# A four-layer conditioned transformer: two small norm operations from POOL to DVE, the norm's scalings on ACT seven pieces behind them, row transpositions nine pieces behind their load

## The chip, the cores and the metric

The kernel runs on one core of one Trainium2 chip, as one program that holds all four layers. Engines are called PE (TensorE), DVE (VectorE), ACT (ScalarE), POOL (GpSimd) and SP (SyncE, which issues most DMAs here). The metric is the device time of one launch in microseconds; the time before is the median of six runs. L12 is line 12 of the kernel before.

## The reference, cut to what matters

There are 4 batches of 512 tokens with 288 channels, and a condition vector for each batch. Each layer does the same two halves; the six modulation rows of a layer come from the condition.

```python
def layer(x, c, ...):                       # x (4, 512, 288), c (4, 288)
    mod = silu(c) @ ada_w + ada_b           # (4, 6 * 288)
    shift_a, scale_a, gate_a, shift_m, scale_m, gate_m = split(mod, 6, axis=-1)
    norm = lambda x: (x - mean(x)) / sqrt(var(x) + 1e-6)     # over channels
    h = norm(x) * (1 + scale_a) + shift_a
    x = x + gate_a * (attention(h) @ proj_w + proj_b)
    h = norm(x) * (1 + scale_m) + shift_m
    return x + gate_m * mlp(h)              # 288 -> 1152, gelu, -> 288
```

All layers have 16 heads of 18 channels. Layers 0, 1 and 3 attend over the 512 tokens of a batch. Layer 0 has four experts of which each token takes two; the others have a plain MLP. Layer 2 attends, inside each token, over its 16 heads, and then reads its result in another order:

```python
    attn = softmax(einsum("nthd,ntkd->nthk", q * scale, k))   # 16 x 16 in each token
    out = einsum("nthk,ntkd->nthd", attn, v)
    out = out.transpose(0, 2, 1, 3).reshape(n, t, d)          # heads before tokens
```

So a row of what goes into layer 2's projection holds parts of many tokens: the kernel writes the attention's result to memory and loads it back as rows.

## The kernel before, in words

**Tiles.** Tokens lie on partitions: 16 tiles of 128 tokens, four tiles (TB) for each batch b = 0 to 3; `x` with all of them stays in SBUF. For the products the normalised tokens are transposed into `ht`, channels on partitions: 3 chunks of 96 (first half of a layer) or 128 (second half).

**Planner.** The kernel writes down all engines' instructions in an order that it works out itself while it is built. PE's main work (steps of the attention, blocks of an MLP) is written by plain loops, which call `gap()` at set places. One gap is one turn of the planner: its clock `flow["now"]` goes one up, and in it side work is written down behind what stands there already. Side work is a Python generator; what it yields is a cost in us by the planner's own tables, or `WAIT` (no more of this generator in this turn; the text calls such a turn a piece behind), or `BANK` (it goes on when the turn's one free PSUM bank is its own). A wait of this kind is a place in the written order, not an instruction: each engine works off its queue in that order, and semaphores see to the rest. `mark(key, n)` says that a key counts as ready n turns on, and generators and loops wait for keys in turns as well.

**Where the change lies.** From 1298.1 us (the first L982), at the tail of layer 1's attention, layer 2's attention runs beside what is left of layer 1, the MLPs from 1327.3 us on (the first L1849). PE's loop is `half_mlp`: the MLPs of layer 1's batches 2 and 3 and then of layer 2's four batches, each batch in two halves of 256 tokens with 18 gaps a half (up L1849 and the remainder's channels, gelu L1860 on ACT, down L1871, then L1882 to L1884). Layer 2's MLP of batch b may begin only when its `ht` and the gate rows are there; until then the loop writes empty gaps:

```python
for b in range(B):
    while any(ready.get(key, 1 << 30) > flow["now"] for key in (("ht", 2, 1, b), ("gate", 2, 1))):
        gap(0.5)
```

Two lists are advanced once per gap by `follow()`, with a credit of 1.6 us a gap. `chain` is `stream()` in `attention_over_heads`: for 16 tiles in turn, products q, k, v of a tile (`kept`, matmuls L982 on PE, copy L991 on ACT), scores (`weigh`, DVE L1000 and L1006), maxima and shift (L1010 DVE, L1011 POOL), exponentials (L1155 ACT, of two tiles at once), sums of weights (L1034, L1035), values times weights (`weighted`, L1018, mostly on POOL), their sums (L1030 DVE), the division (L1043) and the write to memory (L1044, a DMA on SP). `beside` holds, for each batch, `before(b)`: the first norm of layer 2 and its chunks; and `after(b)`, which starts when batch b's last tile is written: `read(b)` (the DMA that loads the rows, and a memset on POOL), three transpositions of rows (`turned`, L1061 on PE, L1062 on ACT), four projections (`project`, L1068 PE, L1072 ACT, L1073 and L1074 POOL), and then the second norm and its chunks. A turn gives its bank to one of them, to `beside` before `chain`. Rows and the chunks' scratch tile share the buffers of `ht`; the normalised tokens `xh` have one buffer, which `norm` waits for in turns (`held`).

**The norm.** `norm(l, half, b)` takes statistics on DVE (L507, L508: one pair per tile), and has three forms. The form for layer 2 and for layer 3's first half (`scalar`) makes 1/sqrt(var + eps) and -mean/sqrt(var + eps) in four small operations on POOL over all four tiles at once (128x4 values), yields `WAIT` three times, takes `xh`, and then has ACT scale the four tiles (L532: `xh = x * rstd + off`). POOL then fills the columns behind the 288 (a copy L551 for second halves, a memset L556 for first halves), and `xh` counts as ready four turns on. The other form has DVE L522 for the eps, the same 128x4 operation as POOL's L515. `chunks` transposes `xh` on PE (L575) and modulates on ACT (L576). While layers 1 and 3 attend over tokens, the norms of batches go through another list, `lanes`, that has two turns per attention step. Twelve norms have the scalar form. Their first scalings begin at 1217.2, 1315.1 (layer 2, first half, batches 0 and 1), 1439.2 (the same, batch 2), 1489.3 (second half, batch 0), 1504.8 (first half, batch 3), 1571.6 (second half, batch 1), 1607.3 (layer 3, batch 0), 1658.3 and 1731.1 (layer 2, second half, batches 2 and 3), and 1812.2, 1826.1 and 1850.7 (layer 3, batches 1 to 3).

Other lines that the steps name: L264, L620 and L621 are memsets on POOL for layer 3's attention; the gate rows of layer 2's second half are loaded by one DMA and count as ready 8 turns after it is issued; L1407, L1717 and L1726 belong to layer 0's experts.

Of the kernel before, what the change touches and what calls it, by code (L numbers as in the profile page):

```python
# [12 lines left out]
ALU = mybir.AluOpType  # L13
# [16 lines left out]
EPS = 1e-6  # L30
# [29 lines left out]
def tile_dit_blocks(ctx: ExitStack, tc: tile.TileContext, x_in, cond_t, sel_den, sel_b, w_gate, layers, out):  # L60
# [14 lines left out]
    nc = tc.nc  # L75
# [28 lines left out]
    def mark(key, delay=1):  # L104
        ready[key] = flow["now"] + delay
# [395 lines left out]
    def norm(l, half, b):  # L501
        key = (l, half, b)
        n = f"{l}_{half}_{b}"
        mv = small.tile([P, TB, 2], F32, tag="mv", name=f"mv_{n}")
        for t in range(TB):
            st = small.tile([P, 6], F32, tag="st", bufs=4, name=f"st_{n}_{t}")
            nc.vector.bn_stats(st, x[:, b * TB + t, :])  # L507
            nc.vector.bn_aggr(mv[:, t, :], st)  # L508
            yield 0.6
        rstd = small.tile([P, TB], F32, tag="rstd", name=f"rstd_{n}")  # L510
        scalar = (l, half) in ((OVER_HEADS, 0), (OVER_HEADS, 1), (OVER_HEADS + 1, 0))
        if scalar:

            off = small.tile([P, TB], F32, tag="off", name=f"off_{n}")
            nc.gpsimd.tensor_scalar_add(rstd, mv[:, :, 1], EPS)  # L515
            nc.gpsimd.tensor_tensor(rstd, rstd, minus_half, ALU.pow)
            nc.gpsimd.tensor_tensor(off, mv[:, :, 0], rstd, ALU.mult)
            nc.gpsimd.tensor_scalar_mul(off, off, -1.0)
            for _ in range(3):
                yield WAIT  # L520
        else:
            nc.vector.tensor_scalar_add(rstd, mv[:, :, 1], EPS)  # L522
            nc.gpsimd.tensor_tensor(rstd, rstd, minus_half, ALU.pow)
        while held:
            yield WAIT
        held.append(key)
        xh[key] = work.tile([P, TB, CX], F32, tag="xh", bufs=1, name=f"xh_{n}")
        yield 0.0 if scalar else 0.6
        for t in range(TB):
            to = xh[key][:, t, :C]  # L530
            if scalar:
                nc.scalar.activation(  # L532
                    to, x[:, b * TB + t, :], AF.Identity, bias=off[:, t : t + 1], scale=rstd[:, t : t + 1]
                )
            elif (l, half) == (0, 1):

                add, scale = tokens_mod[b]
                nc.vector.scalar_tensor_tensor(
                    to, x[:, b * TB + t, :], mv[:, t, 0:1], scale, ALU.subtract, ALU.mult
                )  # L540
                nc.vector.scalar_tensor_tensor(to, to, rstd[:, t : t + 1], add, ALU.mult, ALU.add)
            else:
                nc.vector.tensor_scalar(
                    to, x[:, b * TB + t, :], mv[:, t, 0:1], rstd[:, t : t + 1], ALU.subtract, ALU.mult
                )
            if t < TB - 1:
                yield 0.1 if scalar else 0.6
        if (l, half) == (0, 1):
            pass
        elif half == 1:  # L550
            nc.gpsimd.tensor_copy(  # L551
                xh[key][:, :, C:].rearrange("p t (r c) -> p t r c", c=RC),
                xh[key][:, :, KF * P : C].unsqueeze(2).to_broadcast([P, TB, NR - 1, RC]),
            )
        else:
            nc.gpsimd.memset(xh[key][:, :, C : C + 1], 1.0)  # L556
        mark(("xh",) + key, 4 if scalar else 3)
        yield 0.1 if scalar else 0.6
# [40 lines left out]
    def attention(l, start):  # L599
# [298 lines left out]
        for b in range(B):  # L898
# [4 lines left out]
                lanes, start - 70 if first else at_step(s0 - LEAD - 9 if b else s0 - LEAD - 6),  # L903
                [("x", l, 0, b)] + ([("scattered", B - 1)] if l == 1 else []) + ([("step", l, 0)] if b else []),
                norm(l, 0, b),
            )
            free = [("first products", l, b - 2)] if b >= 2 else []
# [54 lines left out]
    def attention_over_heads(l):  # L962
# [83 lines left out]
        def read(b):  # L1046
            rows = work.tile([P, TB, C + 1], F32, tag="rows", bufs=1, name=f"rows_{l}_{b}")
            nc.sync.dma_start(
                rows[:, :, :C],
                scratch[b].rearrange("h t d -> (h t d)").rearrange("(n p c) -> p n c", p=P, c=C),  # L1050
            )
            nc.gpsimd.memset(rows[:, :, C : C + 1], 1.0)
            xh["rows", b] = rows

        def turned(b, k):
            if k == 0:
                rt[b] = work.tile([P, NK, S], F32, tag="ht", bufs=2, name=f"rt_{l}_{b}")
            n = KP + (1 if k == NK - 1 else 0)
            to = other()
            for t in range(TB):  # L1060
                nc.tensor.transpose(to[:n, t * P : (t + 1) * P], xh["rows", b][:, t, k * KP : k * KP + n], ident)  # L1061
            nc.scalar.copy(rt[b][:n, k, :], to[:n, :])  # L1062

        def project(b, t):
            pp = other()[:, :C]
            for k in range(NK):
                n = KP + (1 if k == NK - 1 else 0)
                nc.tensor.matmul(  # L1068
                    pp, rt[b][:n, k, t * P : (t + 1) * P], w["wp"][:n, k, :], start=k == 0, stop=k == NK - 1
                )  # L1070
            upd = work.tile([P, 2, C], F32, tag="upd", bufs=2, name=f"upd_a_{l}_{b}_{t}")
            nc.scalar.copy(upd[:, 0, :], pp)  # L1072
            nc.gpsimd.tensor_tensor(upd[:, 0, :], upd[:, 0, :], gates[l, 0][:, b, :], ALU.mult)  # L1073
            nc.gpsimd.tensor_tensor(x[:, b * TB + t, :], x[:, b * TB + t, :], upd[:, 0, :], ALU.add)  # L1074

        def until(*keys):
            while any(ready.get(key, 1 << 30) > flow["now"] for key in keys):
                yield WAIT

        def turn_normed(half, b):  # L1080
            yield from until(("mod", l, half), ("xh", l, half, b))
            turn = chunks(l, half, b)
            for k in range(NK):
                yield BANK
                next(turn)
                yield -0.9

        def before(b):

            yield from until(("x", l, 0, b))  # L1090
            if b >= 2:
                yield from until(("first products", l, b - 2))
            yield from norm(l, 0, b)
            yield from turn_normed(0, b)

        def after(b):

            for _ in range(3):
                yield WAIT
            read(b)  # L1100
            for _ in range(6):
                yield WAIT
            yield from until(("gate", l, 0), ("projection", l))
            for k in range(NK):
                yield BANK
                turned(b, k)
                yield -0.9
            for t in range(TB):
                yield BANK
                project(b, t)  # L1110
                yield -1.5
            mark(("x", l, 1, b), 4)
            yield from until(("x", l, 1, b))
            yield from norm(l, 1, b)
            yield from turn_normed(1, b)

        def stream():
# [13 lines left out]
            def second(behind=2):  # L1131

                k = at["weighted"]
                cost = 0.0
                if k < 4 * at["weighed"]:
                    if k % 4 == 0:
                        denominators(k // 4)
                        cost += 0.7
                    weighted(k // 4, k % 4)
                    at["weighted"] += 1  # L1140
                k = at["summed"]
                if k < at["weighted"] - behind:
                    summed(k // 4, k % 4)
                    at["summed"] += 1
                    cost += 1.4
                    if k % 4 == 3:
                        finish(k // 4)
                        if k // 4 % TB == TB - 1:
                            beside.append([after(k // 4 // TB), False])
                return cost  # L1150
# [992 lines left out]
```

## Time and profile before

| | |
|---|---|
| median of 6 runs | 2280.57 us (2274.94 to 2295.01) |
| the profiled execution | 2294.54 us |
| its span in the profile | 2292.5 us, mean granted TensorE clock 0.966 |
| PE | 2131.6 us busy, 93% of the span, 11018 matmuls |
| PEld | 1202.1 us, 52% |
| DVE | 1063.9 us, 46% |
| ACT | 807.2 us, 35% |
| POOL | 523.9 us, 23% |

A line of a timeline reads: start in us from the span's begin, duration, engine, line, operation, output and inputs by the program's tile names, their shapes, how many instructions were put together (x4), and in brackets how long the engine had stood idle before it and what ended that. PE is the matmuls, PEld the weight loads that overlap them. The slices of the page cut the span in 40 parts of 57.3 us; a digit is the busy share of one part in tenths. Matmul ends are modelled, so a PE that is shown busy is not one at its peak.

### The profile page before, as it was taken

The page shows a single profiled execution, that of the slowest core. Times are in us where ns is not written, and L with a number is a line of the kernel's source. Part 1 is how long each engine was busy: PE and PEld are TensorE (multiplying, and loading weights), DVE is VectorE, ACT ScalarE, POOL GpSimd, SP SyncE. Part 2 cuts the span into 40 slices and gives each one's busy share as a digit, 9 for nine tenths or more (in the row PEclk, how much of TensorE's full clock was granted, in tenths as well). Part 3 has the DMA queues.
Part 4 walks back from the last instruction along what each step waited for, and adds up shares of the span by engine and source line. Part 5 has one row for each costly group of instructions (what it writes and reads, how often), then busy time and mean ns, then how long its engine had stood idle before and what let it go on. Part 6 is the DMA issues. An engine that isn't in the chain of part 4 may idle for free.

```text
span 2292.5 us, 29720 instructions
## 1 busy us (share of the span) xinstructions
PE 2131.6 (93%) x11018; PEld 1202.1 (52%) x11018; DVE 1063.9 (46%) x1638; ACT 807.2 (35%) x1275; POOL 523.9 (23%) x553
## 2 busy tenths in 40 slices
PE   7889999999999999899999999989789999999998
PEld 3334434467775676344444566666556444443555
DVE  4546666540022212466535269898711455555111
ACT  2433434422221122445425322433312554445110
POOL 2001021230021120110001119898931200001000
PEclk9989999999999899999999989999989999999999
DMA  3243212346564463100000000210201100000000
GB/s 71 85 124 127 85 43 59 88 135 183 173 194 124 128 191 117 37 24 22 11 9 24 1 17 8 65 31 9 37 26 42 49 23 12 14 21 1 1 21 21
DMA packets 176066, 140.52 MB, mean 61 GB/s; under 512 B 83201, under 2 KB 157773, under 8 KB 175922
## 3 DMA queue, kind: packets, MB, share of 16 engines
q1 hardware_dynamic: 172654, 128.87, 19.8%
q0 software_dynamic: 3072, 9.44, 1.2%
q8 instruction: 88, 1.44, 0.3%
q14 instruction: 56, 0.46, 0.1%
q10 hardware_dynamic: 196, 0.31, 0.0%
HBM read 97.56 MB, written 26.29 MB: 54 GB/s over the span
## 4 chain that ended last, share of the span: by engine, by line
PE 63%; DVE 11%; POOL 4%; DMA 2%; issue 2%; ACT 2%; another core or an unknown queue 0%; SPq 0%; POOLq 0%; ACTq 0%; DVEq 0%
PE banks L705 12%; PE banks L634 7%; PE banks L1665 7%; PE banks L1645 6%; PE banks L1812 5%; DVE mx L715 4%; PE banks L1789 4%; PE banks L811 4%; PE banks L769 4%; PE banks L1871 2%; PE banks L1849 2%; POOL pv L1018 2%; DVE pq L1000 2%; PE banks L1651 1%; DVE ho L1030 1%
## 5 line engine op out<-in xcount | busy, mean ns | idle before, releaser
L715 DVE TENSOR_REDUCE mx<-banks 128x4 f32<-128x2048 f32 (+1 forms) x354 | 423.3, 1236 | 371.8 <-PE banks L705 343.8
L743 ACT ACTIVATE ex<-banks 128x1024 f32<-128x1024 f32 (+1 forms) x471 | 377.8, 865 | 360.0 <-PE banks L705 357.1
L705 PE MATMUL banks<-qk 32*128 32x512 f32 x3072 | 446.7, 633 | 52.7 <-DVE mx L715 18.4
L705 PEld LDWEIGHTS banks<-qk 32*128 32x128 f32 x3072 | 171.2, 187 | 227.6 <-issue 86.7
L1018 POOL TENSOR_TENSOR pv<-hs,qk 128x1152 f32<-128x1152 f32 x60 | 192.7, 3224 | 11.0 <-ACT hs L1155 11.0
L769 PE MATMUL banks<-ex,va 128*32 128x512 f32 x1536 | 191.9, 611 | 2.3 <-ACT ex L743 2.3
L1665 PE MATMUL banks<-w_b,hid_b 128*128 128x288 f32 x684 | 190.2, 423 | 0.0
L634 PE MATMUL banks<-ht,wqk 96*128 96x512 f32 (+1 forms) x348 | 172.4, 630 | 3.3 <-DVE mx L715 3.2
L1645 PE MATMUL banks<-block,w_b 128*128 128x256 f32 x684 | 166.0, 389 | 0.6 <-ACT hid_b L1657 0.6
L1657 ACT ACTIVATE hid_b<-banks,b_b 128x256 f32<-128x256 f32 x171 | 68.7, 471 | 273.8 <-PE banks L1651 164.7
L1665 PEld LDWEIGHTS banks<-w_b,hid_b 128*128 128x128 f32 x684 | 125.6, 193 | 55.3 <-issue 26.9
L1645 PEld LDWEIGHTS banks<-block,w_b 128*128 128x128 f32 x684 | 130.7, 195 | 28.2 <-issue 8.7
L794 POOL COPY rec<-r 128x512 f32<-128x512 f32 x48 | 29.9, 623 | 445.7 <-DVE r L790 431.5
L1871 PE MATMUL banks<-w,hid 128*128 128x288 f32 x432 | 128.5, 433 | 0.0
L1849 PE MATMUL banks<-ht,w 128*128 128x256 f32 x432 | 111.7, 393 | 17.8 <-ACT hid L1860 17.4
L769 PEld LDWEIGHTS banks<-ex,va 128*32 128x32 f32 x1536 | 39.9, 110 | 138.2 <-issue 69.4
L593 POOL TENSOR_TENSOR x<-x,upd_a 128x288 f32<-128x288 f32 x48 | 38.0, 793 | 322.0 <-DVE upd_a L592 307.8
L811 PE MATMUL banks<-wp,ot 128*128 128x288 f32 x384 | 106.3, 423 | 5.6 <-DVE mx L715 3.1
L1812 PE MATMUL banks<-w,hid 128*128 128x288 f32 x432 | 108.8, 410 | 0.0
L634 PEld LDWEIGHTS banks<-ht,wqk 96*128 96x128 f32 (+1 forms) x348 | 63.6, 194 | 83.6 <-issue 58.3
L1849 PEld LDWEIGHTS banks<-ht,w 128*128 128x128 f32 x432 | 82.1, 195 | 38.9 <-ACT hid L1860 22.2
L1789 PE MATMUL banks<-ht,w 128*128 128x512 f32 x216 | 97.2, 595 | 3.4 <-ACT hid L1805 2.3
(225 smaller groups left out, 2469.5 us busy)
## 6 DMA issues: line engine op xcount, KB each, us to landing
w_b<-in_w SPq DMA_DIRECT2D x57, 432.0 KB
w_b<-in_w SPq DMA_DIRECT2D x57, 384.0 KB
qk<-qc SPq DMA_DIRECT2D x316, 38.0 KB
wa<-in_wada SPq DMA_DIRECT2D x24, 288.0 KB
block<-x_mem SPq DMA_DIRECT2D x19, 288.0 KB
y_mem<-y_b SPq DMA_DIRECT2D x19, 288.0 KB
x_mem<-zeros SPq DMA_DIRECT2D x21, 256.0 KB
y_mem<-zeros SPq DMA_DIRECT2D x21, 256.0 KB
```

The costliest lines, as they stand in the source:

```text
L634: nc.tensor.matmul(to, st(rows, k), mv(rows, k), start=k == 0, stop=k == NK - 1)
L705: nc.tensor.matmul(to, qk[u][r, of, c * P : (c + 1) * P], qk[u][r, 1 - of, :], start=True, stop=True)
L715: nc.vector.tensor_reduce(mxs[u % 2][:, c, j : j + n], banks[:, bank + j : bank + j + n, :], AX.X, ALU.max)
L743: nc.scalar.activation(ex[step, j // 2][:, j % 2 : j % 2 + n, :], banks[:, to[j] : to[j] + n, :], AF.Exp)
L769: nc.tensor.matmul(to[j * HP : (j + 1) * HP, :], vas[0][:, c, at : at + HP], ex[step, j // 2][:, j % 2, :], start=first, stop=last,)
L811: nc.tensor.matmul(pp, done[b * NG + g][:, t * P : (t + 1) * P], w["wp"][:, g, :], start=g == 0, stop=g == NG - 1)
L1018: engine.tensor_tensor(prod, sc[i][:, hs, :].unsqueeze(2).to_broadcast([P, GH, HD, NH]), qkv[i][:, 1].rearrange("p h d -> p d h").unsqueez ...
L1645: nc.tensor.matmul(banks[:, UP + j, :BT], w1[:, k, j * P : (j + 1) * P], hx[i][:, k, :], start=k == 0, stop=False)
L1665: nc.tensor.matmul(banks[:, PY + t, :C], hid[j][:, t * P : (t + 1) * P], w2[:, j, :], start=f == 0, stop=f == NF - 1)
L1789: nc.tensor.matmul(banks[:, 4 + j, :], full[:, k, (f % 3) * P : (f % 3 + 1) * P], h[:, k, :], start=k == 0, stop=False,)
L1812: nc.tensor.matmul(banks[:, t, :C], hf[:, t * P : (t + 1) * P], w["w2"][f // 3][:, f % 3, :], start=f == 0, stop=f == NF - 1,)
L1849: nc.tensor.matmul(banks[:, UP + j, :BT], full[:, k, (f % 3) * P : (f % 3 + 1) * P], h[:, k, s], start=k == 0, stop=False,)
```

## The change

In the scalar form of the norm, the addition of eps goes from POOL to DVE. The sign change, which was done on the product on POOL, is now done on the mean, on DVE, before the product. POOL keeps the power and the product. Seven `WAIT`s instead of three stand between these operations and the four scalings on ACT. In `after(b)`, nine `WAIT`s instead of six stand between the load of the rows and their transpositions. Nothing else differs.

```diff
@@ norm, scalar form
-            nc.gpsimd.tensor_scalar_add(rstd, mv[:, :, 1], EPS)
+            nc.vector.tensor_scalar_add(rstd, mv[:, :, 1], EPS)
+            nc.vector.tensor_scalar_mul(off, mv[:, :, 0], -1.0)
             nc.gpsimd.tensor_tensor(rstd, rstd, minus_half, ALU.pow)
-            nc.gpsimd.tensor_tensor(off, mv[:, :, 0], rstd, ALU.mult)
-            nc.gpsimd.tensor_scalar_mul(off, off, -1.0)
-            for _ in range(3):
+            nc.gpsimd.tensor_tensor(off, off, rstd, ALU.mult)
+            for _ in range(7):
                 yield WAIT
@@ after(b)
             read(b)
-            for _ in range(6):
+            for _ in range(9):
                 yield WAIT
```

## The prediction

> **What bounds the kernel now.** I read the page's slices first. PE is near full throughout; DVE and POOL are full together only around slices 24 to 28, so the changed lines, which run from 1210 to 1852 us, matter mostly there.
>
> ```profile
> PE   7889999999999999899999999989789999999998
> DVE  4546666540022212466535269898711455555111
> POOL 2001021230021120110001119898931200001000
> ```
>
> Next, windows cut where PE's MLP work of batches starts and stops (columns: stretch, length, then busy time of PE, PEld, DVE, ACT, POOL, granted clock, DMA).
>
> ```profile
> 1436.00:1488.70 52.70, 48.01 (x217) 35.04 (x216) 43.16 (x50) 20.05 (x37) 45.38 (x35) 1.00 0.29 71
> 1488.70:1507.30 18.60, 11.36 (x42) 7.28 (x41) 18.29 (x24) 7.83 (x14) 17.11 (x13) 0.80 0.26 40
> 1507.30:1585.30 78.00, 74.34 (x313) 54.03 (x313) 72.43 (x72) 28.88 (x53) 73.85 (x45) 0.94 0.12 18
> 1585.30:1654.80 69.50, 59.54 (x255) 42.21 (x253) 51.65 (x61) 23.47 (x43) 62.49 (x47) 0.95 0.24 30
> 1654.80:1671.00 16.20, 7.85 (x19) 4.09 (x20) 10.57 (x8) 4.87 (x8) 15.22 (x17) 0.68 0.16 19
> ```
>
> From 1671 to 1797 PE works off the last two MLP batches alone, 119.36 of 126.00 us busy. So the stage ends when PE has done its work plus its pauses before 1671; rows two and five are the places where it has no MLP to do and waits for the norm of the next batch. Last, the engines' timelines: the scalings (L532) on ACT, and what PE shows behind them.
>
> ```profile
> 1439.19 2.19 ACT L532 ACTIVATE xh<-x,off,rstd 128x288 f32<-128x288 f32 x4 [3.25 <-POOL off L518]
> 1504.81 2.19 ACT L532 ACTIVATE xh<-x,off,rstd 128x288 f32<-128x288 f32 x4 [6.91 <-POOL off L518]
> 1571.64 2.19 ACT L532 ACTIVATE xh<-x,off,rstd 128x288 f32<-128x288 f32 x4 [6.67 <-POOL off L518]
> 1607.29 2.18 ACT L532 ACTIVATE xh<-x,off,rstd 128x288 f32<-128x288 f32 x4 [5.62 <-POOL off L518]
> 1658.31 2.19 ACT L532 ACTIVATE xh<-x,off,rstd 128x288 f32<-128x288 f32 x4 [8.38 <-POOL off L518]
> ```
>
> ```profile
> 1505.49 2.01 PE L575 MATMUL banks<-ident,xh 128*96 128x128 f32 x4 [3.93 <-ACT xh L532]
> 1574.54 1.82 PE L1849 MATMUL banks<-ht,w 128*128 128x256 f32 x4 [0.33 <-ACT hid L1860]
> 1609.89 1.13 PE L1849 MATMUL banks<-ht,w 128*128 128x256 f32 x4 [2.52 <-ACT hid L1860]
> 1616.29 1.09 PE L1061 MATMUL banks<-ident,rows 128*96 128x128 f32 x4 [3.48 <-DMA rows<-scratch]
> 1658.99 0.33 PE L575 MATMUL banks<-ident,xh 128*128 128x128 f32 x1 [4.23 <-ACT xh L532]
> ```
>
> ACT stands 31.0 us in six such waits. Behind L532 in its queue are the MLP's activations (L1860) and the copies L991, and PE then waits for those, or for xh itself.
>
> **Parts: the two operations.** In the six norms between 1436 and 1660 POOL loses L515 and L518, 0.31 and 0.23 us with the step between, 3.3 us in all. DVE gains two operations of 0.165 (L522, the same 128x4 form), 0.33 x 6 = 2.0 us; DVE is 93% busy in the third row, so I count them whole. They can be held: DVE's 128x288 TENSOR_SCALAR (L1717) took 0.36 us when it began first, and 1.51 when a POOL operation of 1.50 had begun.
>
> ```profile
> 665.26 1.51 DVE L1717 TENSOR_SCALAR outs<-outs,shares 128x288 f32<-128x288 f32 x1
> ```
> ```profile
> 665.10 1.50 POOL L1726 TENSOR_TENSOR x<-x,outs 128x576 f32<-128x576 f32 x1
> ```
>
> Behind POOL's products (L1018, 3.2 us) the hold per norm lies between 0 and 2 x 3.2. POOL itself sat waiting for DVE's statistics at three of the six L515 and had at most 0.6 us of other work left at the others, so I take 1.0 for all six. The page "SBUF — State Buffer" of the Trainium skill, "Who interferes with whom", makes a rule of it that speaks against this change: tensor_scalar on two ports and a GpSimd operation exclude each other for the whole instruction. By the rule's worst order at every norm the six would cost DVE 38 us.
>
> **The scalings.** A gap is one turn of the planner. A half MLP has 18 gaps and took 36.7 us (its first ones-products at 1388.51 and 1425.17), 2.04 us each; the wait of row two is 13 gaps, 1.43 each. Four gaps more are 8.2 us inside the MLP and 5.7 in a wait: more than every ACT stall except the 6.91 (1.2 left) and, barely, the 8.38. What goes: pauses of 1.66 (1443), 2.52 (1609) and 1.1 (1572, four short ones and 0.33), and at 1574 matmuls at half speed (L1849 x4 1.82 against 1.03; six groups, 3.5 over): 8.8. In row two 3.93 and (2.01-0.60)+(1.91-1.03) of slow matmuls: 6.2. In row five 4.23+0.38: 4.6. The page "TensorE: Matmul & The Clock Gate", Part 1, puts the slow clock behind an idle window of about 3.4 us; the pauses at 1572 were shorter, so by it the 3.5 would not be the scalings' and the gain would be 3.5 less. The slow rows directly behind them decide for me.
>
> **The row transpositions.** read() and its DMA stay where they are; only L1061 goes three gaps back, 6.1 us. Pauses 1.48, 0.34 and 3.48 (5.3); I take 4.5, since the third batch's row load shares SP's queue with the next layer's weights. Also, DVE idles 8.89 us before 1475.04, until L982: tile 8's three products stand behind the seven bank pieces of after(0) (three transpositions, four projections, PE 1456 to 1471). Batch 2's chunks end at the fourth gap later than now, and two gaps then remain before those seven: tile 8 fits in, tile 9 waits instead. Between 0 and 8.9; I take 3.0, since the exponentials (L1155) move back with tile 9.
>
> **What is late next.** From the projection to the next MLP: x counts as written after 4 gaps, statistics 1 or 2, waits 3 (now 7), 1 to take xh, 4 until xh counts, 3 chunks, 1. Row two ends not with that but with the gate load, 8 gaps after x; the chunk has 5 gaps of slack, so 7 later is 2 beyond: 15 gaps. Batch 1 has no slack now (no pause at 1585): 7 later less those 2 is 5. Batch 2: own chain 7 later, MLP start 7 later: 4 gaps become 3 or 4. Sum +6 gaps at 1.43 = 8.6. PE pays for these only if it runs out of other work; half of them hold L982 and transpositions that move there, but I count all. At the end POOL's copy L551 falls behind the memsets L264, L620 and L621 (3.61+1.15+0.21); less the 3.3 saved, 1.7.
>
> **Attention stages.** For the norms at 1210 and from 1803 on, four more turns are two steps, some 10 us. The chunks at 1820.84 go to about 1831 and the first two products of batch 1 into the same step; its keys are needed some 20 us on. Nothing on POOL stalls ACT there. Counted at zero; if the cover is short, one wait for a spread, 8.0 us (DMA qk<-qc at 1674.70).
>
> **Sum.** Gains 8.8+6.2+4.6+4.5+3.0 = 27.1; costs 8.6+2.0+1.0+1.7 = 13.3, and 0.8 for what is left of the two longest stalls: 13.0 net. The profiled execution was 2294.54 (span 2292.5), 14.0 above the median 2280.57; there it would give 2281.5. Off the median: 2267.5.
>
> **Rivals.** (1) The waiting is only handed on. DVE is 18.29 of 18.60 busy in row two and POOL 15.22 of 16.20 in row five; if these engines' own chain, not ACT's order, sets when xh is there, the 6.2+4.6+3.0 don't come: -13.0+13.8 = +0.8, near 2281; with half, 2274. For it: POOL itself waits 21.6 us at L515 for statistics. Against: ACT's stalls ended in L1849 pauses inside the MLP, where nothing needed the norm yet. (2) Slower: the gaps become the wait. If the chain of batch 1 keeps its order against PE, PE stands out 7 gaps (2+5) at the MLP's 2.04 us, +14.3, and nothing of rows two and five returns, while 8.8+4.5 inside the MLP is lost again to copies (L991) that now come before POOL has freed their tile; 2294.9. It decides when PE reaches the first chunk of batch 1 with xh unwritten by more than 6 us; for it, the zero slack at 1585; against, PE reaches that point earlier than now only by what it gained. (3) It doesn't do what it says: DVE's pair held at each norm by 3.2, 19 us on a full DVE; that eats the gain, 2280 or so.
>
> **Numbers.** A measurement of this kernel can tell about 0.5%, 11.4 us, from no change. Stalls go and most of it is kept: 0.62, of it 0.44 beyond 11.4 (own range 2256 to 2277). Rivals 1 and 3 together: 0.23, of it 0.19 within, 0.02 on either side. Rival 2: 0.15, of it 0.13 slower. Faster 0.46, same 0.39, slower 0.15. Low 2253: all gains, half the gaps hidden (4.3), tile 8 wholly (5.9), -23 and some noise of the median. High 2291: most of rival 2.
>
> **What would show it.** Right: L532 waits under 3 us in all where there were 31.0; L1061 waits under 1.5 where 5.3; no slow group near 1574; PE before the last two batches done some 13 us sooner; the pause before the first chunk of MLP batch 1 (now none) 2 to 5 us. DVE's two operations near 0.17 and not 1 to 3. Wrong: that pause over 8 us, or L991 waiting for L1018 on POOL by over 15 us between 1436 and 1660.

## The result: 0.73% slower, and the profile after

The change runs at 1.0073 of the time before, with a 95% interval of 1.0055 to 1.0092, so it takes about 16.7 us more (the two medians, 2303.47 us and 2284.56 us, lie 18.9 apart). The forecast was 2267.5 us, 13 us less, and its range ended at 2291.0.

The profiled execution took 2300.54 us (span 2298.8, clock 0.963). The two spans differ in layer 0's experts by chance: the 1281st score product (L705) comes at 974.37 us before and at 963.67 after, with nothing of the change ahead of it. I therefore count from a product that both have behind all that, the 1793rd L705 (1187.64 and 1176.97 us). From there to the end it is 1104.9 us before and 1121.9 after, 17.0 more, close to the 16.7 of the ratio. In three steps, each from the start of one instruction to the start of the other: to the last sum of layer 2's attention on DVE (L1030) 478.8 and 477.2; from there to the last down product of layer 2's MLP (L1871) 129.3 and 138.5; from there to the 2561st L705, in layer 3's attention, 151.7 and 161.1. The rest is 345.1 and 345.2. So DVE's chain beside the MLPs ends as early as before, PE needs 9.2 us more from there to its last down product, and layer 3's attention takes 9.4 us more.

The slices of the page after:

```profile
PE   7889999899999999899999898798789899999998
DVE  4545566540022214466443389789530455565111
POOL 2001021230021120110010159788811100001000
```

DVE and POOL are full at the same place as before, and PE's digits there have two 7s where there was one. Windows cut as in the prediction at the starts and stops of PE's MLP work (the same columns; the fifth row is the pause before layer 2's third MLP batch, the sixth the last two batches):

```profile
1421.00:1475.30 54.30, 50.67 (x214) 37.35 (x214) 43.05 (x40) 20.91 (x39) 47.75 (x29) 0.91 0.32 71
1475.30:1497.00 21.70, 6.76 (x18) 4.32 (x19) 21.18 (x36) 6.67 (x12) 16.64 (x14) 0.58 0.09 28
1497.00:1572.00 75.00, 71.94 (x318) 53.51 (x317) 65.56 (x69) 28.31 (x53) 65.99 (x39) 0.96 0.10 16
1572.00:1664.70 92.70, 72.00 (x264) 48.58 (x263) 69.36 (x74) 26.46 (x49) 79.67 (x60) 0.83 0.23 34
1664.70:1688.50 23.80, 14.10 (x45) 7.58 (x43) 4.14 (x7) 3.29 (x5) 0.00 (x0) 0.71 0.08 29
1688.50:1792.60 104.10, 104.10 (x470) 72.23 (x470) 14.23 (x30) 26.61 (x56) 19.17 (x19) 1.00 0.14 42
```

Length less busy time is PE's idle time: 3.6, 14.9, 3.1, 20.7, 9.7 and 0.0, in all 52.0 us. Before, the five rows and the last stretch had 4.7, 7.2, 3.7, 10.0, 8.4 and 6.6, in all 40.5. The second row doubled, and so did the fourth, batch 1's MLP.

A longer pause is not yet a loss, though. Counted from the first mark, layer 2's MLP of batch 0 starts at 319.7 us before and at 320.0 after, and that of batch 1 at 397.7 and 395.0: row two begins 2.7 us sooner than before and holds 4.6 us less work, and nothing is late at its end. The time is lost behind that, between the start of batch 1's MLP and that of the third (483.3 us before, 511.6 after). PE idles 30.4 us there where it idled 18.3. About 15 us more of that stretch is other work done sooner: from the third MLP on, PE has 104.1 us of work left in place of 119.4.

ACT's waits, from the view of waits between the first L982 and the last L1871 (columns: who waits for whom, us in total, times, longest):

```profile
ACT qk L991 <- POOL pv L1018: 20.9, 7, 8.4
ACT upd_a L1072 <- POOL x L1074: 14.9, 2, 8.2
ACT xh L532 <- POOL off L518: 7.9, 1, 7.9
ACT upd_m L1882 <- POOL x L1074: 5.1, 1, 5.1
ACT hs L1155 <- POOL hs L1011: 5.0, 4, 2.2
```

The scalings' wait that the prediction was built on fell from 31.0 to 7.9 us. But ACT waits for POOL still: with a last group of 2.7 (L991 for L556) these are 56.5 us, and the same view before has 60.4 (31.0 for L518, 11.6 and 10.8 in the first two groups, 7.0 in four small ones). The waits of PE in the same stretch:

```profile
PE banks L1849 <- ACT hid L1860: 25.5, 6, 11.6
PE banks L575 <- POOL xh L551: 7.8, 1, 7.8
PE banks L705 <- ACT qc L660: 6.3, 1, 6.3
PE banks L575 <- ACT xh L532: 6.1, 1, 6.1
PE banks L705 <- DMA qk<-qc: 3.4, 2, 3.2
```

Before, L1849 waited for the gelu 11 times, 17.4 us together and never over 2.8; now six times, with one of 11.6. How that one comes about is to be read from the engines' timelines, ACT first, then POOL and PE:

```profile
1623.44 0.40 ACT L1072 COPY upd_a<-banks 128x288 f32<-128x288 f32 x1 [8.15 <-POOL x L1074]
1630.59 0.40 ACT L1072 COPY upd_a<-banks 128x288 f32<-128x288 f32 x1 [6.75 <-POOL x L1074]
1632.30 0.84 ACT L1860 ACTIVATE hid<-banks,b 128x256 f32<-128x256 f32 x2
```

```profile
1623.37 3.13 POOL L1018 TENSOR_TENSOR pv<-hs,qk 128x1152 f32<-128x1152 f32 x1
1626.45 0.68 POOL L1043 TENSOR_TENSOR ho<-ho,hd 128x288 f32<-128x288 f32 x1
1627.09 0.80 POOL L1073 TENSOR_TENSOR upd_a<-upd_a,gate 128x288 f32<-128x288 f32 x1
1627.96 2.60 POOL L1074 TENSOR_TENSOR x<-x,upd_a 128x288 f32<-128x288 f32 x1
```

```profile
1632.83 3.48 PE L1849 MATMUL banks<-ht,w 128*128 128x256 f32 x8 [11.58 <-ACT hid L1860]
1681.82 2.04 PE L705 MATMUL banks<-qk 32*128 32x512 f32 x2 [3.20 <-DMA qk<-qc]
1683.79 1.54 PE L575 MATMUL banks<-ident,xh 128*128 128x128 f32 x6
```

The third batch's projections have two tiles `upd` for their copies, and POOL frees one only with L1074, behind its products L1018. The gelu of batch 1's MLP stands on ACT behind the waiting copies, and PE behind the gelu. The last two lines are the start of the third MLP: its chunk (L575) stands on PE behind layer 3's first score products, and these wait for the spread's DMAs. In the kernel before, the gelu that follows the third batch's projections, and the first of layer 3's score products, read

```profile
1638.63 2.79 PE L1849 MATMUL banks<-ht,w 128*128 128x256 f32 x8 [2.37 <-ACT hid L1860]
1684.40 1.12 PE L705 MATMUL banks<-qk 32*128 32x512 f32 x2
```

and the third MLP's chunk came ahead of that L705, at 1658.99.

### The profile page after: what moved, and what is told of

It reads as the page before. It is cut to its first block, busy times and chain, and to the rows that moved or that the text cites. A ratio compares the mean times of both kernels' runs of the same rounds, so it can differ in the third digit from the quotient of the medians.

```text
span 2298.8 us, 29740 instructions
## 1 busy us (share of the span) xinstructions
PE 2124.4 (92%) x11018; PEld 1200.0 (52%) x11018; DVE 1071.6 (47%) x1662; ACT 806.4 (35%) x1274; POOL 518.0 (23%) x529
## 3 DMA queue, kind: packets, MB, share of 16 engines
q1 hardware_dynamic: 172654, 128.87, 19.6%
## 4 chain that ended last, share of the span: by engine, by line
PE 63%; DVE 12%; POOL 3%; issue 2%; DMA 2%; ACT 2%; another core or an unknown queue 0%; SPq 0%; POOLq 0%; DVEq 0%; ACTq 0%
PE banks L705 12%; PE banks L1665 7%; PE banks L634 7%; PE banks L1645 6%; PE banks L1812 5%; DVE mx L715 4%; PE banks L1789 4%; PE banks L811 4%; PE banks L769 3%; PE banks L1871 3%; PE banks L1849 2%; DVE pq L1000 2%; DVE ho L1030 2%; POOL pv L1018 2%; PE banks L1651 1%
## 5 line engine op out<-in xcount | busy, mean ns | idle before, releaser
L705 PE MATMUL banks<-qk 32*128 32x512 f32 x3072 | 446.1, 632 | 58.4 <-DVE mx L715 19.2
L705 PEld LDWEIGHTS banks<-qk 32*128 32x128 f32 x3072 | 171.0, 186 | 235.9 <-issue 87.5
L1018 POOL TENSOR_TENSOR pv<-hs,qk 128x1152 f32<-128x1152 f32 x60 | 190.6, 3189 | 8.8 <-ACT hs L1155 8.8
L634 PE MATMUL banks<-ht,wqk 96*128 96x512 f32 (+1 forms) x348 | 170.3, 624 | 3.3 <-DVE mx L715 3.2
L1665 PEld LDWEIGHTS banks<-w_b,hid_b 128*128 128x128 f32 x684 | 124.0, 190 | 52.9 <-issue 25.1
L1849 PE MATMUL banks<-ht,w 128*128 128x256 f32 x432 | 114.4, 401 | 26.3 <-ACT hid L1860 25.5
L1871 PE MATMUL banks<-w,hid 128*128 128x288 f32 x432 | 129.5, 435 | 0.0
L1849 PEld LDWEIGHTS banks<-ht,w 128*128 128x128 f32 x432 | 84.9, 201 | 47.3 <-ACT hid L1860 28.3
L634 PEld LDWEIGHTS banks<-ht,wqk 96*128 96x128 f32 (+1 forms) x348 | 62.9, 192 | 83.1 <-issue 57.1
```

The costliest lines, as they stand in the source:

```text
L634: nc.tensor.matmul(to, st(rows, k), mv(rows, k), start=k == 0, stop=k == NK - 1)
L705: nc.tensor.matmul(to, qk[u][r, of, c * P : (c + 1) * P], qk[u][r, 1 - of, :], start=True, stop=True)
L1018: engine.tensor_tensor(prod, sc[i][:, hs, :].unsqueeze(2).to_broadcast([P, GH, HD, NH]), qkv[i][:, 1].rearrange("p h d -> p d h").unsqueez ...
L1665: nc.tensor.matmul(banks[:, PY + t, :C], hid[j][:, t * P : (t + 1) * P], w2[:, j, :], start=f == 0, stop=f == NF - 1)
L1849: nc.tensor.matmul(banks[:, UP + j, :BT], full[:, k, (f % 3) * P : (f % 3 + 1) * P], h[:, k, s], start=k == 0, stop=False,)
L1871: nc.tensor.matmul(banks[:, PY + t, :C], hf[:, t * P : (t + 1) * P], w["w2"][f // 3][:, f % 3, :], start=False, stop=f == NF - 1,)
```

## The experiments

All ratios are to the kernel before, measured beside each other, with 95% intervals. The last four columns come from each kernel's profile, in us, with the marks used above: to the last L1030, on to the last L1871, on to the 2561st L705, and from the first mark to the end. One profile is one execution: the last column goes with the ratio to about 5 us in every row but e_dve's, which is 7.2 us longer than before's where the ratio says 2.3 shorter.

| kernel | ratio | L1030 | L1871 | L705 | to the end |
|---|---|---|---|---|---|
| before | 1 | 478.8 | 129.3 | 151.7 | 1104.9 |
| the change | 1.0073 [1.0055, 1.0092] | 477.2 | 138.5 | 161.1 | 1121.9 |
| e_dve | 0.9990 [0.9975, 1.0004] | 484.9 | 127.7 | 154.3 | 1112.1 |
| e_r9 | 0.9988 [0.9974, 1.0002] | 479.0 | 129.7 | 151.7 | 1105.4 |
| e_w7 | 1.0079 [1.0057, 1.0100] | 485.2 | 134.8 | 159.1 | 1124.6 |
| e_dve_w7 | 1.0087 [1.0065, 1.0110] | 484.3 | 135.8 | 159.1 | 1124.3 |
| e_dve_r9 | 0.9982 [0.9969, 0.9995] | 478.5 | 128.6 | 152.4 | 1104.7 |
| e_l3only | 0.9993 [0.9981, 1.0004] | 478.3 | 126.2 | 158.4 | 1108.1 |
| e_h1only | 1.0036 [1.0023, 1.0049] | 479.8 | 139.4 | 151.7 | 1116.1 |
| e_h0only | 0.9968 [0.9954, 0.9981] | 476.2 | 127.8 | 152.3 | 1101.5 |
| e_l2only | 1.0044 [1.0029, 1.0060] | 479.0 | 139.8 | 151.7 | 1115.6 |
| e_pair | 1.0077 [1.0055, 1.0099] | 477.5 | 142.0 | 161.0 | 1125.7 |
| e_h0_pair | 0.9986 [0.9973, 1.0000] | 476.2 | 127.7 | 152.4 | 1101.4 |
| e_h0_h1w1 | 1.0023 [1.0007, 1.0039] | 477.1 | 137.4 | 151.7 | 1111.4 |
| e_hold | 1.0046 [1.0029, 1.0064] | 477.3 | 136.4 | 159.2 | 1118.0 |
| e_holds | 1.0046 [1.0030, 1.0061] | 477.4 | 134.8 | 160.0 | 1117.4 |
| e_holds_pair | 1.0047 [1.0029, 1.0064] | 477.5 | 134.7 | 160.0 | 1117.4 |
| e_h0_30 | 0.9966 [0.9954, 0.9979] | 476.3 | 126.0 | 151.7 | 1099.1 |
| e_copy | 1.0057 [1.0022, 1.0091] | 477.5 | 138.9 | 157.6 | 1119.1 |
| e_three | 1.0017 [0.9988, 1.0046] | 478.5 | 133.8 | 154.2 | 1111.8 |

**Each edit alone.** Edits against the kernel before: e_dve has only the four lines of the operations, e_w7 only the first of these lines, e_r9 only the second, e_dve_w7 the operations and the first.

```diff
-            for _ in range(3):      # norm, ahead of the scalings
+            for _ in range(7):
-            for _ in range(6):      # after(b), behind read(b)
+            for _ in range(9):
```

> Only the two operations on DVE; three turns before the scalings and six before the row transpositions, as before. Theory 1 (the time comes from the written order: the turns put copies on ACT and a copy on POOL behind other work; the operations themselves cost 0.33 us a norm): 0 to 3 us faster than before, L532's waits for POOL's product fall from 31.0 by some 3 us, MLP batch starts unchanged. Theory 2 (the two operations stand in DVE's full queue, and POOL's power now waits behind them): 10 us or more slower, POOL's waits for DVE at the power over 10 us above those of before.

> Only the seven turns before the scalings; the four operations on POOL and six turns before the row transpositions as before. Theory 1: 8 to 18 us slower: the pause before layer 2's first MLP chunk grows from 6.5 to about 14 us since POOL's copy into xh (L551) stands behind the next norm's operations, the copies L991 wait for POOL's products over 15 us, and layer 3's attention takes some 9 us more. Theory 2: within 5 us of before.

> Only the nine turns between row load and row transpositions. Theory 1: 3 to 10 us slower, with PE idle about 10 us more behind the third batch's projections, whose copies on ACT (L1072) wait for POOL's x (L1074); layer 3's attention unchanged. Theory 2: 0 to 5 us faster, from L1061's 5.3 us of waits for the rows.

> The whole change except that six turns stay before the row transpositions. Theory 1: slower than before by what seven turns alone cost, less 0 to 3 us: 6 to 16 us. Theory 2: slower by 10 us or more, the same as the two operations alone. If nearly all of the change's cost of about 17 us is in the nine turns, this one is within 5 us of before.

The two operations on DVE come out 0.10% faster and the nine turns 0.12%; neither interval excludes 1. Seven turns alone cost 0.79%, the whole of it. Theory 2, DVE's queue, is out. Theory 1 had the seven turns right, though e_dve_w7 is some 20 us slower where it allowed 16, and the nine wrong. In e_r9 no L1061 waits for the rows any more (11.1 us in the line's view before), and the time is 0.12% less: the pauses of 5.3 us on PE came back elsewhere, L532 waits 40.2 us there where it waited 31.0, and L1849 waits 21.1 us for the gelu where it waited 17.4.

**By norm.** The base is e_dve_r9 (operations and nine turns, three turns at the norms); the others give seven turns to one group of norms.

```diff
-            for _ in range(3):
+            for _ in range(7 if l > OVER_HEADS else 3):                # e_l3only
+            for _ in range(7 if half == 1 else 3):                     # e_h1only
+            for _ in range(7 if l == OVER_HEADS and half == 0 else 3): # e_h0only
+            for _ in range(7 if l == OVER_HEADS else 3):               # e_l2only
```

> Two operations on DVE and nine turns before the row transpositions, but three turns before the scalings as before: the base of the next three. Alone these parts gave ratios of 0.9990 and 0.9988. If they add up: 0.9978, some 5 us faster than before. If nine turns gain only by cover that the two operations also use up: 0.999.

> As the base (two operations on DVE, nine turns), with seven turns for layer 3's first norms only, three for layer 2's. Theory A (part of the cost is the norms inside layer 3's attention, where four turns more put chunks and key products behind two further steps): 7 to 10 us above the base, of it 7.5 to 9.4 between the end of layer 2's last MLP and the 2560th score product, and PE's idle time there near 10 where before had 7.4. Theory B (that stretch is longer because of what the MLP stage leaves over for it): within 3 us of the base.

> As the base, with seven turns for layer 2's second norms only (the ones that the next MLP waits for). Theory C (the MLP waits for the longer chain: xh later, MLP start later by four turns a batch): 8 us or more above the base, the pauses at the MLP starts grow, the copies L991 wait for POOL's products no longer than before (11.6 us). Theory D (the first norms move tile products in front of POOL's products): within 3 us of the base.

> As the base, with seven turns for layer 2's first norms only. Theory C: within 3 us of the base, or faster, since nothing of the MLPs waits for these norms. Theory D: 6 us or more above the base, the copies L991 wait for POOL's products over 20 us where before had 11.6, and the pause near the start of the second half of layer 1's last MLP is about 7 us where it was 2.8.

> The whole change, with layer 3's norms back at three turns. The whole stood at 1.0073 of before. If layer 3's turns cost in the whole what its trace shows between the last MLP of layer 2 and the 2560th score product (160.6 us against 151.3 to 152.0 where layer 3 has three turns): 6 to 9 us less, 1.0033 to 1.0047, and that stretch back at 151 to 152 us. If they cost only the 2.5 us by which they alone stood over the base: 1.006.

The second norms of layer 2 cost 0.54% over the base, 12 us; in the profiles it is 11.4, of it 10.8 between the last L1030 and the last L1871. That is theory C's size, but not its account: L991 waits 19.1 us for POOL in e_h1only, where C had it no longer than the 11.6 of before. Layer 2's first norms come out 0.14% below the base, within the intervals, although the first pause that Theory D named is there (6.80 us) and L991 waits 16.2 us for POOL: D is out. Layer 3's turns cost 6 us inside the attention and gain 2.4 in front of it; in the whole change the attention's stretch is 161.1 us with them and 151.7 without (e_l2only), and the ratios differ by 0.29%, 6.6 us. What the attention pays for is on PE after, 35 us into it:

```profile
1829.78 1.46 PE L705 MATMUL banks<-qk 32*128 32x512 f32 x2 [2.00 <-DMA qk<-qc]
1831.17 3.23 PE L769 MATMUL banks<-ex,va 128*32 128x512 f32 x16
```

The chunks of batch 1 come two steps later (L575 41.7 us behind the last L1871 in place of 25.1), new pauses of 0.63, 0.64 and 2.00 us appear before score products and a transposition of maxima, and behind the last one the same 16 value products that take 1.92 us elsewhere take 3.23: the granted clock is 0.66 between 1830 and 1835. Of the 9.4 us between 151.7 and 161.1, 2.7 are something else: twelve products at the start of that stretch ran at a slow clock, behind pauses that both kernels have (the last section has the lines). e_l3only has no such slow products and stands at 158.4; e_dve and e_three have them with three turns, and stand at 154.3 and 154.2.

**The longest pause taken away.** Against the change (e_pair) and against e_h0only (e_h0_pair), two projections share a tile, so the copies have four places:

```diff
-            upd = work.tile([P, 2, C], F32, tag="upd", bufs=2, ...)
-            nc.scalar.copy(upd[:, 0, :], pp)
+            if t % 2 == 0:
+                xh["pair", b] = work.tile([P, 2, C], F32, tag="upd", bufs=2, ...)
+            upd = xh["pair", b]
+            nc.scalar.copy(upd[:, t % 2, :], pp)
...                                  # POOL's two operations on upd[:, t % 2, :]
```

> The whole change; besides, two projections of a batch share one tile of two rows, so that ACT's copies L1072 have four places where they had two, and no longer wait for POOL's x (L1074) of two projections before. Theory E (the 11.58 us pause behind the third batch's projections is on the path): 5 to 12 us faster than the whole change, 1.002 to 1.005 of before, that pause under 4 us. Theory F (POOL and DVE set the pace there, and PE waits later for what it gains): within 3 us of the whole change, 1.006 to 1.0085.

> The fastest kernel so far (two operations on DVE, nine turns, seven turns for layer 2's first norms only; 0.9968) with the same shared tiles. Theory E: 3 to 8 us faster than that, 0.9935 to 0.9955, since L1072 waited 18.8 us for POOL there and PE stood 1.80 and 3.23 us behind it. Theory F: 0.996 to 0.998.

Theory E is out in both. e_pair lies in theory F's range; e_h0_pair is a little slower than F had it. PE in e_pair, whose lines behind this edit have numbers two higher:

```profile
1606.10 1.99 PE L1851 MATMUL banks<-ht,w 128*128 128x256 f32 x8 [0.73 <-ACT hid L1862]
1614.94 1.33 PE L1870 MATMUL banks<-b,ones 1*128 1x288 f32 x4 [6.21 <-ACT upd_m L1884]
1655.46 2.04 PE L705 MATMUL banks<-qk 32*128 32x512 f32 x2 [10.25 <-DMA qk<-qc]
1661.32 2.46 PE L705 MATMUL banks<-qk 32*128 32x512 f32 x4 [3.82 <-ACT qc L660]
1666.52 2.04 PE L705 MATMUL banks<-qk 32*128 32x512 f32 x2 [2.73 <-DMA qk<-qc]
```

The 11.58 became 0.73. The wait for the third batch's rows, ahead of it, grew from 3.30 to 7.35. Nine us behind it PE waits 6.21 for the next copy behind the same POOL, and at the third MLP's start 16.8 where it waited 9.7.

**Fewer turns, and the order at the third MLP.** e_h0_h1w1 is e_h0only with one turn at layer 2's second norms. e_hold and e_holds are the change with an added condition; e_holds_pair has the shared tiles as well. e_h0_30 is e_h0only with seven turns also for layer 3's batch 0.

```diff
# e_hold: score products ahead of layer 3's attention
-                ..., [("spread", l, u)], ahead(step, c))
+                ..., [("spread", l, u)] + ([("ht", prev, 1, 2)] if prev == OVER_HEADS else []), ahead(step, c))
# e_holds: its first spread
-                        [("packed", l, b, m) for m in blocks] + free + ["cleared"] + ...
+                        ... + ["cleared"] + ([("ht", prev, 1, 2)] if prev == OVER_HEADS and u == 0 else []) + ...
```

> The fastest kernel so far with one turn instead of three for layer 2's second norms. If each turn there costs by delaying the next MLP (12 us for four): 4 to 6 us faster, 0.9942 to 0.995. If seven turns there cost by what the pieces meet, not by their number: no such trend, between 3 us faster and 8 us slower (0.9955 to 1.0003), with L532's waits for POOL's product above the 37.2 us of that kernel.

> The whole change; besides, layer 3's first score products also wait until the chunks of layer 2's third MLP are written, so that PE has L575 before L705. Theory G (the order of these two is what the second norms' turns cost): 5 to 9 us faster than the whole change, 1.0033 to 1.005, the chunks' transpositions some 8 us earlier than the first L705, and the pauses before L705 at that MLP's start (6.26 + 3.20) gone or beside MLP work. Less if ACT's spread DMAs (10.24 us from the first to the last) still hold the chunks' copies L576. Theory F (PE stands there for POOL and the DMAs in any order): 1.006 to 1.0085.

> The whole change; besides, layer 3's first spread waits for the chunks of layer 2's third MLP, so that ACT has L576 before its five DMAs and PE L575 before L705. Theory G: 8 to 14 us faster than the whole change, 1.001 to 1.0037, that MLP starts 10 us or more earlier. Theory F: 1.006 to 1.0085, since layer 3's first score products are late then and PE waits for them after the MLPs.

> The same as the one before, with the projections' copies in shared tiles as well. If the two causes lie one behind the other (the pause behind the projections was hidden behind the spread when it was taken away alone): 5 to 10 us faster than the run with the spread alone. If not: within 3 us of it.

> The fastest kernel so far (0.9968), with seven turns also for layer 3's norm of batch 0, which lies in the MLP stage; batches 1 to 3 keep three. If layer 3's turns gain there what the run with layer 3 alone showed (2.6 us of the MLP stage) and lose only inside the attention: 2 to 3 us faster than that, 0.9955 to 0.996, and 151 to 153 us from the last MLP to the 2560th score product. If batch 0's turns are what the attention pays for: that stretch at 158 us, 0.998 to 1.000.

One turn at the second norms is 0.55% worse than three, as seven is, and so slower than either outcome that I had named: their number is not a price. e_hold gains 0.27% over the change, at the edge of what the intervals tell apart; in the profiles, which agree with each other to 0.1 us from the first mark to the start of batch 1's MLP, it is 3.9 us. Of these, 2.0 come up to the last L1871, and 1.9 in the attention, whose first products do not meet the slow clock here. PE in e_hold:

```profile
1663.64 2.82 PE L575 MATMUL banks<-ident,xh 128*128 128x128 f32 x12 [5.78 <-ACT qc L660]
1667.95 3.88 PE L705 MATMUL banks<-qk 32*128 32x512 f32 x8 [1.49 <-ACT qc L660]
```

The chunk stands first now, but its bank is freed by a copy (L660) that ACT does behind the spread's DMAs. In the fast e_h0only the same place reads

```profile
1632.02 0.33 PE L575 MATMUL banks<-ident,xh 128*128 128x128 f32 x1 [3.33 <-ACT xh L532]
1654.38 1.14 PE L705 MATMUL banks<-qk 32*128 32x512 f32 x8
```

with the chunk 22 us ahead of the score products. e_holds held only unit 0's spread; unit 1's score products still stood in front of L575 and waited 4.9 us, so it did not do all that was expected of it, and came out at the same 1.0046, between the two ranges named; in its profile the last L1871 comes 3.5 us sooner than in the change. The shared tiles on top gave nothing. e_h0_30 has the shortest stretch of all (1099.1) and layer 3's attention at 151.7: batch 0's turns do not cost there, batches 1 to 3 pay. By the ratios it can't be told from e_h0only. These two are faster than both kernels of the case, by 0.32 to 0.34% against before.

**The pause at the first MLP start.** e_copy is the change with the copy of the scalar form on ACT; e_three is e_l2only with this and e_holds' condition.

```diff
-            nc.gpsimd.tensor_copy(
+            (nc.scalar.copy if scalar else nc.gpsimd.tensor_copy)(
                 xh[key][:, :, C:].rearrange("p t (r c) -> p t r c", c=RC),
```

> The whole change, with the copy into the columns behind xh's 288 (L551) on ACT, directly behind the four scalings, instead of POOL. Theory H (that copy's place on POOL makes the pause of 7.85 us): the pause goes to under 2 us, 3 to 6 us faster than the whole change, 1.0045 to 1.006. Theory F (POOL and DVE set the pace of that stretch): the pause moves to the next product, 1.0065 or more.

> The whole change with three things taken away at once: layer 3's turns at three, layer 3's first spread behind the third MLP's chunks, the copy on ACT. If these three are where the time went: 1.0073 less 0.0029, 0.0027 and some 0.002, so 0.998 to 1.001, about the kernel with three turns and the other two edits (0.9982). If seven turns at layer 2's norms cost for another reason: 1.003 or more.

What the edit takes away, on POOL after: the copy L551 comes behind the next norm's power and product, and the power waits for DVE's statistics of that norm.

```profile
1488.48 1.01 POOL L517 TENSOR_TENSOR rstd<-rstd,minus_half 128x4 f32<-128x4 f32 x1 [4.65 <-DVE off L516]
1492.81 0.39 POOL L551 COPY xh<-xh 128x256 f32<-128x256 f32 x1
```

PE in e_copy, the pause of 7.82 before it gone, and the next one at that MLP:

```profile
1485.82 1.97 PE L575 MATMUL banks<-ident,xh 128*128 128x128 f32 x8 [0.90 <-ACT qk L991]
1507.29 2.07 PE L1849 MATMUL banks<-ht,w 128*128 128x256 f32 x4 [7.93 <-ACT hid L1860]
```

The first MLP began 7.4 us sooner, and its second half began where it did in the change, to 0.2 us: what was saved was waited for behind a copy L991 and an exponential that POOL's products hold. The pause went as theory H said, and the ratio (1.0057) lies in H's range, but its interval holds the whole change's 1.0073 as well. The profile shows the handing on: up to the last L1871 it is 0.7 us longer than the change's, and the 2.8 us by which it is shorter in all lie in the attention. e_three is 10.1 us shorter than the change in its profile, of it 6.8 in the attention; 1.0017 lies between the two outcomes that I had named, and can't be told from 1.

## Why the prediction was wrong, step by step

- **"The stage ends when PE has done its work plus its pauses": the sentence holds, what I took from it does not.** I took every pause behind an L532 wait as time that goes with the wait, 19.6 us in three places. The waits did go (31.0 to 7.9). PE's idle time in these stretches rose by 11.5. ACT waits for POOL because POOL works through the attention of layer 2, which ends 477 to 479 us behind the mark with and without the change. A piece that no longer waits in one place lets PE come sooner to the next copy that POOL holds. e_pair and e_copy show it with one pause each: 11.58 and 7.82 us taken away, no time gained in that stage. That is rival 1's mechanism, which had 0.23 together with rival 3, and its price was not bounded by zero as I had it. (Of the 21.6 us of POOL's waits that I named for it, 15.0 are one wait at 1729 us, behind the stage.)
- **"What is late next" counted gaps.** In the order as written the empty gaps before layer 2's MLPs are 16 before, 24 in the change, 22 in e_dve_r9 and 26 in e_h0only. So the count was near, 8 more where the sum had 6, and the price of 1.43 us a gap (8.6 in the sum) was wrong: the kernel with the most gaps is among the fastest, and e_w7, a slow one, has 18. What had one is which piece meets which: the third batch's projections beside POOL's last products, the third MLP's chunk behind layer 3's score products (2.0 us of e_hold's profile), the copy into xh behind the next norm's statistics.
- **"Attention stages: counted at zero"** was wrong by 6.7 us in e_l3only's profile and 6.6 by e_l2only's ratio; the 9.4 us of the change's own profile hold 2.7 of the slow clock besides. The 8.0 us that I set against it, one wait for a spread, came near in size by luck: only 2.00 us of what was paid is a wait for a spread, the rest is shorter pauses and products at a slow clock.
- **The two operations** were to come out near nothing, 3.3 us of gain against 3.0 of cost, and they did: e_dve is 0.10% faster, which can't be told from none. The longest L515 there is 0.56 us. In the whole change the hold that I put at 1.0 us came to about 3.9, so the term was too small: ten of the twelve L515 took 0.145 to 0.171 us, one 1.26 and one 2.95. The last began when a POOL product of 3.17 had run for 0.25 us. The rule of the Trainium skill ("SBUF — State Buffer", "Who interferes with whom") is thus borne out in kind; its worst order at every norm was not met, since POOL mostly stood waiting for these operations.
- **The row transpositions** were to give 4.5 and 3.0. Alone they gave 0.12%, 2.7 us, which can't be told from none; in the whole change the third batch still waits 3.30 us for its rows.
- **Rival 2** had nearly the size (+14.3) and not the place. The pause before batch 1's first chunk was to grow past 6 us; there is none, and 0.52 before the last of its three chunks.
- **The signs that I named.** L532 under 3 us: 7.9. PE ready for the last two batches 13 us sooner: it comes 28 us later, counted from the mark (511.6 us in place of 483.3), with 15 us less of other work left. L991 waiting for L1018 over 15 us was the sign for wrong, and it came, 20.9; yet e_h0only has 16.2 and is fast, so that sign was not the cause either.

What stays open: of the 12 us that seven turns at layer 2's second norms cost, the profiles of e_hold and e_holds put 2.0 to 3.5 on the order at the third MLP's start (their ratios 6, at the edge of what the intervals tell apart). The rest lies behind the start of batch 1's MLP, where pauses taken away singly came back; which order of pieces would avoid it was not tried beyond the kernels above.

## What to carry to other kernels

Where one engine's queue paces a stage, a wait on another engine that is taken away comes back at the next piece that the pacing engine holds; before it is counted as gain, look up what the freed engine meets next, and what is left to do when the pacing chain ends. In a kernel whose order is planned by turns, a shift of some turns is a new order: price it by the pairs of pieces that change places, not by turns, and try it for each user of the shift apart, since the same shift cost 0.54% at layer 2's second norms here and nothing at its first. Marks that both profiles pass, at the same count of the same instruction, take the chance differences of an early stage out of the comparison.

## What the runs showed of the hardware

Two things I had not expected. The hold between DVE and POOL goes the other way too: POOL's L1074, 0.79 us elsewhere, took 2.60 at 1627.96 while DVE's own L1018 ran from 1627.81 to 1629.90, and it is part of the 11.58 us pause; the section on interference named above has this case, a DVE instruction with two inputs in SBUF.

```profile
1627.81 2.09 DVE L1018 TENSOR_TENSOR pv<-hs,qk 128x1152 f32<-128x1152 f32 x1
```

And the same pauses do not always cost PE its clock. At the start of layer 3's attention both kernels have pauses of 0.78 and 2.48 us and a third of 0.84 or 0.39. The 8 us from just ahead of the third, and the twelve products L634 behind it, are, first before, then after (columns of the first lines as in the windows above):

```profile
1803.00:1811.00 8.00, 7.16 (x49) 3.88 (x48) 4.79 (x9) 4.51 (x6) 1.75 (x5) 1.00 0.01 3
1804.20 3.18 PE L634 MATMUL banks<-wqk,ht 96*128 96x288 f32 x12 [0.84 <-DVE mx L715]
```
```profile
1800.00:1808.00 8.00, 7.61 (x28) 4.64 (x26) 3.84 (x9) 2.49 (x3) 1.25 (x3) 0.59 0.01 2
1801.14 5.83 PE L634 MATMUL banks<-wqk,ht 96*128 96x288 f32 x12 [0.39 <-DVE mx L715]
```

28 matmuls in 7.61 busy us at a granted clock of 0.59, against 49 in 7.16 at 1.00. Behind the same pause of 2.48 us the twelve products take 3.18 to 3.27 us in 13 of the twenty profiles, 3.79 to 4.00 in three and 5.74 to 5.83 in four. The Trainium skill's page "TensorE: Matmul & The Clock Gate", Part 1, says that the clock goes by activity windows that run freely; no run here shows the windows themselves, but that like pauses fall out differently agrees with it.
